# Attention and ternary FFN on one core: PSUM's banks get fixed roles, and exp scores are taken two heads at a time

## The chip, the cores and the metric

One NeuronCore of a Trainium2 chip runs the whole program. Its engines work in parallel, each through its own instructions in order: TensorE (PE) multiplies matrices and writes its results to PSUM, a memory of eight banks (a bank holds 512 float32 numbers in each of 128 partitions); VectorE (DVE) and ScalarE (ACT) read PSUM; GpSimd (POOL) works on the on-chip memory SBUF; SyncE (SP) issues the DMAs. The metric is the device time of one execution in microseconds; the smaller, the better. Runs are given with their median.

## The reference

The input x has 8 sequences of 1024 tokens with 256 features. Cut to what matters here:

```python
x = x + layernorm(attn(layernorm(x), Wq, Wk, Wv, Wo))
x = x + layernorm(ffn(layernorm(x), weight, alpha, bias))

def attn(x, Wq, Wk, Wv, Wo):            # 16 heads of 16, 4 heads of keys and values
    q, k, v = x @ Wq, x @ Wk, x @ Wv    # q and k are then rotated (rope)
    scores = einsum('bhqd,bhkd->bhqk', q, k) / sqrt(256)
    p = softmax(scores, axis=-1)
    return einsum('bhqk,bhkd->bhqd', p, v) @ Wo

def ffn(y, weight, alpha, bias):        # weight is made ternary: -1, 0 or 1
    return einsum('bsd,od->bso', y, ternary(weight) * alpha) + bias
```

The attention is the large part: 8 sequences, 16 heads and 1024 x 1024 scores for each. The softmax subtracts each row's maximum, so the scores are computed twice here: once to find the maxima, and once, with the maxima subtracted inside the matmul, to take the exponentials.

## The kernel before

**Tiling.** The work is cut into `NU` = 16 units of 512 queries (half a sequence). A unit has `G` = 4 blocks, and a block has the four query heads (one of each key-value head) that share a stacked query tile. A block has `NK` = 8 steps, one for each 128 keys, and a step has four score tiles of 128 keys x 512 queries, one for each head. There are 512 steps and 2048 score tiles. Beside them, the maxima pass has 2048 tiles of 128 queries x 512 keys.

The contraction of a score matmul needs only 64 rows of PE: two heads lie in rows 0 to 63 and 64 to 127 (the letter `a` in the code, the row half), and the other two are chosen with `r2`. Two matmuls on different row halves can run at the same time. Queries and keys are split into a high and a low part that are stacked in these 64 rows, and the rows from 48 on hold the maxima with a factor of -1, so that a score comes out shifted.

**The four kinds of work in the loop.**

- `max_scores` (L565): a maxima matmul (L582, `sm`) into a tile of two banks of the pool `ps_mx`, which has two such tiles. DVE reduces both banks together, or each by itself where a window ends between them (`reduce_halves`, L607; `reduce_early`, L612).
- `shift_join` (L620, DVE), `shift_rows` (L626, a transpose on PE and a copy on ACT) and `shift_low` (L635, DVE and two DMAs) bring the maxima of a finished block into the query rows (`q_st<-ml`).
- `exp_one` (L663): an exp matmul (L655, `se`) into one bank of the pool `ps_e`, which has three, and an `Exp` of 128x512 on ACT (L671). In the last 13 steps `exp_two` (L673) uses the two-bank tiles of `ps_mx`.
- `av_piece` (L683): the exponentials times the values (L691, `av`) into the one bank of `ps_av`; `av_out` copies it to SBUF for a DMA to `d_av`.

So PSUM's banks are 2 x 2 for maxima, 3 for exps and 1 for av.

**The other work.** `Project` computes a unit's queries, keys and values three units ahead; `Tail` computes the output projection, the layer norms and the FFN one unit behind. Their parts stand in the lists `P_PARTS`, `L_PARTS` and `T_PARTS` with the step at which each becomes ready. Each of their PE results takes a bank from `psum` (L183): in the loop one of the three of `ps_e`, before and after it also one of the tiles of `ps_mx`.

**The order.** The order of PE, DVE and ACT is written out by hand: instructions are issued as the code calls them. `window` (L1114) issues two or three score tiles' exps, each followed by a maxima matmul, then the ready parts of other work, and last the av matmuls of the window that lies two windows back (`av_windows`). `window_size` (L1055) takes three tiles, or two where a part that needs a PSUM bank is ready; `do_parts` then lets `3 - size` such parts in. `maxima_by` (L1039) says how far the maxima run ahead of the exps: 40 tiles at first, 52 later. `due` holds finished blocks whose shift is to be sent; `collect` makes it ready on whole steps. The exps of a window come out so (L1124 to L1133):

```python
for q in range(max(size, end - maxima[0])):
    if q < size:
        exp_one(s + q)
    if maxima[0] < end:
        max_scores(maxima[0])
        maxima[0] += 1
```

The SP queue issues the DMAs in the order of the program; POOL's order is written by hand at the start and the end, and follows the parts between.

Of the kernel before, what the change touches and what calls it, by code (L numbers as in the profile page):

```python
# [8 lines left out]
F32 = mybir.dt.float32  # L9
F32R = mybir.dt.float32r  # L10
# [18 lines left out]
def kernel(  # L29
# [48 lines left out]
    ep = ctx.enter_context(tc.tile_pool(name="ep", bufs=12))  # L78
    avp = ctx.enter_context(tc.tile_pool(name="avp", bufs=5))
    tailp = ctx.enter_context(tc.tile_pool(name="tailp", bufs=1))  # L80
    dram = ctx.enter_context(tc.tile_pool(name="dram", bufs=3, space=DRAM))
    ps_mx = ctx.enter_context(tc.tile_pool(name="ps_mx", bufs=2, space=PSUM))
    ps_e = ctx.enter_context(tc.tile_pool(name="ps_e", bufs=3, space=PSUM))
# [97 lines left out]
    spare = [1]  # L181

    def psum(shape, name, dtype=F32):  # L183
        if spare[0]:
            spare[0] += 1
            if spare[0] % 5 < 2:
                return ps_mx.tile(shape, dtype, tag="sm", name=name)
        return ps_e.tile(shape, dtype, tag="se", name=name)
# [116 lines left out]
    class Project:  # L305
# [3 lines left out]
        def __init__(self, u, eng):  # L309
            self.u, self.eng = u, eng  # L310
            self.b, self.half = divmod(u, UPB)
            self.xt, self.sc, self.hl = {}, {}, {}
            self.q_rot = None
            if u not in (1, 2):
                xn = qkp.tile([P, UT, D], F32, tag="xn", name=f"xn_{u}", bufs=2)
                xs = qkp.tile([P, 2, UT, D], F32R, tag="hl", name=f"xs_{u}")
                self.xn = [xn[:, 2 * p : 2 * p + 2, :] for p in range(2)]
                self.xs = [[xs[:, l, 2 * p : 2 * p + 2, :] for l in range(2)] for p in range(2)]
            else:
                self.xn = [  # L320
                    tailp.tile([P, 2, D], F32, tag=f"xn{p}", name=f"xn_{u}_{p}") for p in range(2)
                ]
                self.xs = [
                    [ep.tile([P, 2, D], F32R, tag="e", name=f"xs_{u}_{p}_{l}") for l in range(2)]
                    for p in range(2)
                ]

# [67 lines left out]
        def k(self):  # L395

            pt = psum([P, UQ], f"ptk_{self.u}", F32R)
            for t in range(UT):
                nc.tensor.transpose(
                    pt[:, t * P : (t + 1) * P],  # L400
                    self.k_parts[:, t].rearrange("p l d -> p (l d)"),
                    ident_r,
                )
            self.hl["k"] = ep.tile([P, UQ], F32R, tag="e", name=f"hlk_{self.u}")
            nc.scalar.copy(self.hl["k"], pt.bitcast(F32))
# [156 lines left out]
    def head_and_tile(i, r2, t):  # L562
        return r2 * UT + t if i // G < NU - 1 else 2 * t + r2

    def max_scores(v):  # L565


        i, k = divmod(v // 2, 2 * NK)
        u, part = i // G, v % 2
        if i == 0:  # L570
            a, ch, t, r2 = 1 - part, k // NK, k // 2 % UT, k % 2
        else:
            a, ch, t, r2 = 1 - k % 2, part, k // 4, k // 2 % 2
        queries = block_queries(i, r2)
        queries = queries[:, t * P : (t + 1) * P] if u < NU - 1 else queries[:, t]
        if part == 0:
            sm[0] = ps_mx.tile([P, 2, 512], F32, tag="sm", name=f"sm_{i}_{k}")
            if k == 0:
                mx[i] = small.tile([P, 2, 2 * UT, 2], F32, tag="mx", name=f"mx_{i}")
            reduced.clear()  # L580
        rows = slice(64 * a, 64 * a + 64)
        scores = nc.tensor.matmul(  # L582
            sm[0][:, part, :],
            queries[rows],
            k_st[(u // UPB) % 3][rows, r2, ch * 512 : (ch + 1) * 512],
            start=True,
            stop=True,
        )
        if part == 0:
            return  # L590
        if reduced:
            tc.declare_no_dep(scores.ins, early[0], reason="another bank")
        if i == 0:
            nc.vector.tensor_reduce(
                mx[i][:, ::-1, head_and_tile(i, r2, t), ch], sm[0], AX.X, ALU.max
            )
        else:
            reduce_halves(i, k, 2)
        if k == 2 * NK - 1:
            shift_join(i)  # L600
            due.append((v // 4 + (1 if i < 3 else 2), i))

    def reduce_halves(i, k, n):

        lo = len(reduced)
        a, t, r2 = 1 - k % 2, k // 4, k // 2 % 2
        early[0] = nc.vector.tensor_reduce(  # L607
            mx[i][:, a, head_and_tile(i, r2, t), lo:n], sm[0][:, lo:n, :], AX.X, ALU.max
        ).ins
        reduced.extend(range(lo, n))  # L610

    def reduce_early(v):  # L612

        i, k = divmod(v // 2, 2 * NK)
        if i > 0 and v % 2:
            reduce_halves(i, k, 1)

    sm, mhl, shifts, reduced, early = {}, {}, {}, [], [None]
# [44 lines left out]
    def exp_one(s):  # L663

        n, (a, r2) = s // 4, divmod(s % 4, 2)
        assert n // NK in shifts
        i, kt = divmod(n, NK)
        e = es[n, r2, a] = ep.tile([P, UQ], F32, tag="e", name=f"e_{i}_{kt}_{r2}_{a}")
        sc = ps_e.tile([P, 512], F32, tag="se", name=f"se_{i}_{kt}_{r2}_{a}")
        exp_scores(n, r2, a, sc)  # L670
        nc.scalar.activation(e, sc, AF.Exp, scale=1.0 / D**0.5)  # L671

    def exp_two(n, r2):  # L673

        i, kt = divmod(n, NK)
        sc = ps_mx.tile([P, 2, 512], F32, tag="sm", name=f"se_{i}_{kt}_{r2}")
        for a in range(2):
            exp_scores(n, r2, a, sc[:, a, :])
        for a in range(2):
            e = es[n, r2, a] = ep.tile([P, UQ], F32, tag="e", name=f"e_{i}_{kt}_{r2}_{a}")  # L680
            nc.scalar.activation(e, sc[:, a, :], AF.Exp, scale=1.0 / D**0.5)
# [255 lines left out]
    def load(u):  # L937
# [5 lines left out]
        (26, "begin", 0), (33, "x", 0, 0), (34, "x", 0, 1), (37, "begin", 1), (43, "x", 1, 0),  # L943
        (45, "x", 1, 1), (49, "kv_and_dram"), (51, "q", 0), (52, "kt"), (53, "v"), (55, "q", 1),
        (57, "q_to_dram"),
# [8 lines left out]
        (1, "fetch"), (7, "invert"), (8, "scale", 0), (9, "scale", 1), (12, "attn", 0),  # L954
# [4 lines left out]

    P_FIRST = (47, 51, 52, 54, 57, 58, 59, 60, 62, 61, 63, 64)  # L960
# [24 lines left out]
    for k, fs in enumerate((  # L985
# [26 lines left out]
        for f in fs:  # L1012
            at(k - START, *(f if isinstance(f, tuple) else (f,)))
    for u in range(3, NU):
        start = SPU * (u - 4)
        steps = P_FIRST if u == 3 else [k for k, *_ in P_PARTS]
        at(start + steps[0] - 6, load, u)
        if u == 3:
            for k, stage in (
                (7, measure), (9, prepare_wo), (11, add_up), (13, threshold), (15, ternarize),  # L1020
                (22, transpose_ternary),
            ):
                at(k, stage)
        at(start + steps[0] - 1, begin_project, u)
        for k, (_, *p) in zip(steps, P_PARTS):
            at(start + k, part, projects, u, *p)
# [27 lines left out]

    def window_size(s):  # L1055


        left = 4 * NK - s % (4 * NK)
        if s >= ends:
            return 4  # L1060
        if s == 6:
            return 2
        size = min(2 if s >= REGULAR and any(banked(*p) for p in ready) else 3, left, ends - s)
        if left - size == 1:
            size += 1 if size == 2 else -1
        return size

    maxima = [0]

    def collect(n):  # L1070

        if due and due[0][0] <= maxima_by(4 * n + 4) // 4 - 1:
            i = due.pop(0)[1]
            ready.insert(0, (shift_rows, (i,)))
        ready.extend(todo.pop(n, ()))

    def do_parts(banks):

        while ready:
# [14 lines left out]
    def start_step(n):  # L1094
        for q in range(4):
            max_scores(maxima[0])
            maxima[0] += 1
            if q == 1:
                take_low()
        collect(n)  # L1100
        do_parts(99)
# [12 lines left out]
    def window(s):  # L1114
# [5 lines left out]
        if late:  # L1120
            for r2 in range(2):
                exp_two(s // 4, r2)
        else:
            end = min(maxima_by(s + size), 4 * NSTEP)  # L1124
            for q in range(max(size, end - maxima[0])):
                if q < size:
                    exp_one(s + q)
                if maxima[0] < end:
                    max_scores(maxima[0])
                    maxima[0] += 1  # L1130
                if q == 0:
                    take_low()
            reduce_early(maxima[0])  # L1133
# [10 lines left out]
    with tc.manual_schedule(engines={E.PE, E.DVE, E.Activation, E.Pool}):  # L1144
# [40 lines left out]
        spare[0] = 0  # L1185
# [11 lines left out]
        s = 0  # L1197
        while s < 8:
            s = window(s)
# [6 lines left out]
    spare[0] = 1  # L1206
# [69 lines left out]
```

## Time and profile before

| what | value |
|---|---|
| median of 3 runs | 1646.88 us (1641.69 to 1648.25) |
| profiled execution | 1642.63 us |
| its span | 1640.8 us |
| granted PE clock, mean | 0.989 |
| score matmuls: exps (L655), maxima (L582) | 2048, 2048 |
| first and last exp matmul start | 62.7 and 1618.7 us |

The page gives each engine's busy time as a share of the span, then the chain of work that ended last, then groups of equal instructions with the mean time of one. In a line of a group, the part behind the bar has the busy time in us and the mean duration in ns, then the engine's idle time ahead of these instructions and what ended it. A line of waits says: waiting instruction, the one it waited for, total us, times, the longest. A line of the timeline has the start in us, the time in us, the engine, the line in the code and the operation. PEld is PE's weight load, which can overlap a matmul. Some rows merge equal neighbours (x3, x5). A matmul's end is modelled.

From 100 to 1536 us the loop is regular: in each stretch of 100 us PE is busy for 95 to 99 us, DVE for 82 to 91, ACT for 75 to 81, and the granted clock is 1.00.

### The profile page before, as it was taken

What the parts mean: (1) busy time and instruction counts of PE and PEld (TensorE: products, weight loads), DVE (VectorE), ACT (ScalarE), POOL (GpSimd) and SP (SyncE); (2) the same over time, 40 slices, a digit from 0 to 9 for tenths busy, and PEclk for the clock granted to TensorE, in tenths of its full rate; (3) what the DMA queues carried; (4) which work ended last, traced back from release to release, by engine and by line L of the source; (5) the groups of instructions that cost most, each with busy time, mean ns of one, the idle gap of its engine ahead of it and who ended that gap; (6) DMA issues with size and microseconds to landing.
All of it is one profiled execution on the core that took longest, in us unless ns stands there. A gap on an engine that the chain in (4) does not pass through costs nothing.

```text
span 1640.8 us, 37250 instructions
## 1 busy us (share of the span) xinstructions
PE 1579.7 (96%) x14712; PEld 818.5 (50%) x14712; DVE 1399.3 (85%) x2049; ACT 1274.8 (78%) x2479; POOL 835.4 (51%) x1239
## 2 busy tenths in 40 slices
PE   7999999999999999999999999999999999999997
PEld 5544455454545545454544545455454544444544
DVE  7778788889898888989889898988989888898964
ACT  4657778878787887878788787887878787877884
POOL 5532457374653737455373835547374552323363
PEclk8989999999999999999999999999999999999999
DMA  4151425125151422515133251513325151231100
GB/s 139 53 101 34 91 77 101 59 76 101 56 106 49 91 67 82 101 46 105 60 83 75 77 106 44 104 49 89 71 67 104 40 97 42 46 70 34 42 15 27
DMA packets 86079, 117.99 MB, mean 72 GB/s; under 512 B 12088, under 2 KB 50808, under 8 KB 85752
## 3 DMA queue, kind: packets, MB, share of 16 engines
q1 hardware_dynamic: 85904, 115.60, 29.9%
q8 instruction: 116, 1.90, 0.5%
q14 instruction: 59, 0.48, 0.1%
HBM read 68.65 MB, written 45.88 MB: 70 GB/s over the span
## 4 chain that ended last, share of the span: by engine, by line
PE 80%; DVE 10%; DMA 3%; ACT 2%; POOL 2%; issue 2%; SPq 1%; POOLq 0%; DVEq 0%; ACTq 0%
PE av L691 28%; PE se L655 28%; PE sm L582 9%; DVE mx L607 7%; PE pa L283 3%; PE pq L283 2%; PE pf L283 2%; PE pt_ot L267 2%; ACT e L671 2%; PE pt_xt L267 2%; PE pkv L283 2%; DMA q_st<-ml 1%; DMA k_rot<-d_k 1%; PE pm L630 1%; DMA dk<-ks 1%
## 5 line engine op out<-in xcount | busy, mean ns | idle before, releaser
L607 DVE TENSOR_REDUCE mx<-sm 128x2 f32<-128x1024 f32 (+1 forms) x1304 | 1205.3, 973 | 191.9 <-PE sm L582 174.1
L671 ACT ACTIVATE e<-se 128x512 f32<-128x512 f32 x1996 | 1058.2, 602 | 223.0 <-PE sm L582 172.4
L582 PE MATMUL sm<-k_st,q_st 64*128 64x512 f32 x2048 | 748.4, 450 | 6.9 <-DVE mx L607 3.9
L655 PE MATMUL se<-q_st,k_st 64*128 64x512 f32 x2048 | 705.5, 441 | 26.7 <-ACT e L671 14.4
L691 PE MATMUL av<-e,v_aug 128*32 128x256 f32 (+3 forms) x8608 | 607.2, 378 | 0.0
L655 PEld LDWEIGHTS se<-q_st,k_st 64*128 64x128 f32 x2048 | 324.9, 185 | 405.7 <-ACT e L671 302.1
L582 PEld LDWEIGHTS sm<-k_st,q_st 64*128 64x128 f32 x2048 | 326.1, 185 | 65.1 <-DVE mx L607 41.9
L691 PEld LDWEIGHTS av<-e,v_aug 128*32 128x32 f32 x8608 | 194.4, 108 | 211.0 <-issue 148.3
L241 POOL TENSOR_SCALAR lnsc<-mv 128x2 f32<-128x2 f32 (+1 forms) x134 | 25.8, 193 | 400.1 <-DVE mv L239 395.1
L765 POOL TENSOR_TENSOR xn<-xn,a 128x512 f32<-128x512 f32 x30 | 38.4, 1282 | 131.8 <-DMA a<-d_rec 101.2
L826 POOL TENSOR_TENSOR a<-a,bias_bc 128x512 f32<-128x512 f32 x30 | 38.6, 1287 | 108.3 <-ACT a L825 108.3
L242 POOL TENSOR_TENSOR lnsc<-lnsc,mhalf 128x2 f32<-128x2 f32 (+1 forms) x134 | 92.5, 691 | 0.9
L162 POOL TENSOR_TENSOR hl<-xn,hl 128x512 fp32r<-128x512 f32 x60 | 76.5, 1287 | 0.4
L253 POOL TENSOR_SCALAR xn<-x,lnsc 128x256 f32<-128x256 f32 x116 | 65.1, 570 | 2.2
L237 DVE BATCH_NORM_STATS2 bnst<-a 128x6 f32<-128x256 f32 x120 | 44.5, 413 | 4.6 <-POOL a L826 4.6
L297 POOL TENSOR_TENSOR t<-q_rot,sin_q_sb 128x512 f32<-128x512 f32 x31 | 39.9, 1288 | 15.5 <-ACT q_rot L439 15.4
L283 PE MATMUL pa<-woh,hl 128*128 128x256 f32 x240 | 46.2, 294 | 1.1 <-ACT e L671 1.1
L283 PE MATMUL pq<-xt,wqkvh 128*128 128x256 f32 x256 | 45.8, 303 | 0.5 <-ACT e L671 0.5
L237 DVE BATCH_NORM_STATS2 bnst<-x 128x6 f32<-128x256 f32 x124 | 45.9, 412 | 0.4 <-DMA x<-in_L_attn_x 0.4
L271 ACT CAST ot<-pt_ot 128x512 fp32r<-128x512 f32 x66 | 39.6, 601 | 4.7 <-PE pt_ot L267 4.7
L439 ACT COPY q_rot<-pq 128x512 f32<-128x512 f32 x32 | 18.8, 586 | 30.9 <-PE pq L283 30.9
L162 POOL TENSOR_TENSOR hlq<-q_rot,hlq 128x512 fp32r<-128x512 f32 x31 | 39.8, 1285 | 4.8 <-ACT hlq L159 4.5
(157 smaller groups left out, 1303.1 us busy)
## 6 DMA issues: line engine op xcount, KB each, us to landing
q_st<-dq SPq DMA_DIRECT2D x90, 256.0 KB
dq<-hlq SPq DMA_DIRECT2D x60, 256.0 KB
d_av<-avsb SPq DMA_DIRECT2D x60, 256.0 KB
x<-in_L_attn_x SPq DMA_DIRECT2D x15, 512.0 KB
xn<-d_av SPq DMA_DIRECT2D x30, 256.0 KB
a<-d_rec SPq DMA_DIRECT2D x30, 256.0 KB
xr<-in_L_attn_x SPq DMA_DIRECT2D x15, 512.0 KB
out_x<-a SPq DMA_DIRECT2D x30, 256.0 KB
```

The source lines that it names most:

```text
L162: eng.tensor_tensor(lo, src, hi.bitcast(F32), ALU.subtract)
L237: nc.vector.bn_stats(st[:, t, :], src[:, t, :])
L242: nc.gpsimd.tensor_tensor(sc[:, 1, :], sc[:, 1, :], mhalf[:, :n], ALU.pow)
L253: eng.tensor_scalar(dst[:, t, :], src[:, t, :], sc[:, 0, t : t + 1] if eng is nc.gpsimd else mv[:, t, 0:1], sc[:, 1, t : t + 1], ALU.add i ...
L267: nc.tensor.transpose(pt[:, c, t * P : (t + 1) * P], src[:, t, c * P : (c + 1) * P], ident_r)
L283: nc.tensor.matmul(out, chunk(left[i], c), chunk(right[j], c), start=(k == 0), stop=(k == len(steps) - 1),)
L297: eng.tensor_tensor(dst, x, table.unsqueeze(1).to_broadcast(list(x.shape)), ALU.mult)
L582: scores = nc.tensor.matmul(sm[0][:, part, :], queries[rows], k_st[(u // UPB) % 3][rows, r2, ch * 512 : (ch + 1) * 512], start=True, stop= ...
L607: early[0] = nc.vector.tensor_reduce(mx[i][:, a, head_and_tile(i, r2, t), lo:n], sm[0][:, lo:n, :], AX.X, ALU.max).ins
L655: nc.tensor.matmul(sc if len(queries.shape) == 2 else sc.rearrange("p (j t) -> p j t", j=G), k_st[(i // G // UPB) % 3][rows, r2, kt * P : ...
L671: nc.scalar.activation(e, sc, AF.Exp, scale=1.0 / D**0.5)
L691: nc.tensor.matmul(av_ps[0][32 * r : 32 * r + 32, lo:hi], va[:, kt, r, :], es[i * NK + kt, r // 2, r % 2][:, lo:hi], start=(kt == 0 and lo ...
```

## The change

PSUM's eight banks get fixed roles. `ps_mx` is one tile of two banks for maxima (`s2`), `ps_s` is two single banks for maxima (`s1`), `ps_e` has one tile of two banks for exps (`e2`) and one single bank (`se`), and `ps_av` stays. The single bank takes the third exp of a window of three, and in the loop also the PE results of the other work, which run in windows of two.

A window issues, in this order: the exps of two heads into `e2` (two matmuls on alternate row halves, then one `Exp` of 128x1024), two maxima of the two heads into `s2` (then one reduction of both), and in a window of three the third exp into `se` with a single maximum, on the other row half, into `s1`. The queues `pairs` and `singles` hand out the maxima tiles so that each pair and each single gets the row half that it needs. In the last steps `e2` and `s2` both serve exps.

The exponentials lie in two pools: six tiles of two heads (`ep2`) and four of one (`ep`) for twelve of one; `avsb` has two buffers for five. A shift becomes due a number of maxima tiles after its block, not at whole steps, and is looked for in each window. Some parts of `Project` come some steps later, and two of them are placed behind the newest shift's DMA (`behind_latest`).

```diff
-    ep = ctx.enter_context(tc.tile_pool(name="ep", bufs=12))
-    avp = ctx.enter_context(tc.tile_pool(name="avp", bufs=5))
+    ep = ctx.enter_context(tc.tile_pool(name="ep", bufs=4))
+    ep2 = ctx.enter_context(tc.tile_pool(name="ep2", bufs=6))
+    avp = ctx.enter_context(tc.tile_pool(name="avp", bufs=2))
...
-    ps_mx = ctx.enter_context(tc.tile_pool(name="ps_mx", bufs=2, space=PSUM))
-    ps_e = ctx.enter_context(tc.tile_pool(name="ps_e", bufs=3, space=PSUM))
+    ps_mx = ctx.enter_context(tc.tile_pool(name="ps_mx", bufs=1, space=PSUM))
+    ps_s = ctx.enter_context(tc.tile_pool(name="ps_s", bufs=2, space=PSUM))
+    ps_e = ctx.enter_context(tc.tile_pool(name="ps_e", bufs=1, space=PSUM))
...
-    spare = [1]
+    ALONE, ONE = (ps_e, "se"), (ps_s, "s1")
+    PAIR_E, PAIR_M = (ps_e, "e2"), (ps_mx, "s2")
+    spare = [[ALONE, ONE, PAIR_E, ONE, PAIR_M], 0]
...
+    def max_one(a, sm=None):
+        open_block()
+        if not singles[a]:
+            if pairs:
+                for queue in singles:
+                    queue.append(pairs[0])
+                del pairs[0]
+            else:
+                a = 1 - a
+        i, t, r2, ch = item = singles[a].pop(0)
+        if sm is None:
+            sm = ps_s.tile([P, 512], F32, tag="s1", name=f"s1_{a}_{i}_{t}_{r2}_{ch}")
+        max_scores(item, a, sm)
+        x = head_and_tile(i, r2, t)
+        nc.vector.tensor_reduce(mx[i][:, a, x, ch : ch + 1], sm, AX.X, ALU.max)
+        block_ends(i)
+        return a
+
+    def max_two(a, place=None):
+        open_block()
+        pool, tag = place or PAIR_M
+        sm = pool.tile([P, 2, 512], F32, tag=tag, name=f"s2_{taken[0]}")
...
+        i, t, r2, ch = item = pairs.pop(0)
+        for k in range(2):
+            max_scores(item, (a + k) % 2, sm[:, k])
+        x = head_and_tile(i, r2, t)
+        nc.vector.tensor_reduce(mx[i][:, :: -1 if a else 1, x, ch], sm, AX.X, ALU.max)
+        block_ends(i)
...
-    def exp_one(s):
...
-        sc = ps_e.tile([P, 512], F32, tag="se", name=f"se_{i}_{kt}_{r2}_{a}")
-        exp_scores(n, r2, a, sc)
+    def exps_of(s, n, place=None):
+        pool, tag = place or (ALONE if n == 1 else PAIR_E)
+        shape = [P, 2, 512] if n == 2 else [P, 512]
+        sc = pool.tile(shape, F32, tag=tag, name=f"se_{s}")
+        e = (ep2 if n == 2 else ep).tile(shape, F32, tag=f"e{n}", name=f"e_{s}")
+        for k in range(n):
+            step, (r2, a) = (s + k) // 4, divmod((s + k) % 4, 2)
...
+            exp_scores(step, r2, a, sc[:, k] if n == 2 else sc)
         nc.scalar.activation(e, sc, AF.Exp, scale=1.0 / D**0.5)
...
-            due.append((v // 4 + (1 if i < 3 else 2), i))
+            due.append((taken[0] + (3 if i < 3 else 6), i))
...
     P_PARTS = (
-        (26, "begin", 0), (33, "x", 0, 0), (34, "x", 0, 1), (37, "begin", 1), (43, "x", 1, 0),
-        (45, "x", 1, 1), (49, "kv_and_dram"), (51, "q", 0), (52, "kt"), (53, "v"), (55, "q", 1),
-        (57, "q_to_dram"),
+        (30, "begin", 0), (35, "x", 0, 0), (36, "x", 0, 1), (37, "begin", 1), (43, "x", 1, 0),
+        (45, "x", 1, 1), (49, "kv_and_dram"), (51, "q", 0), (54, "kt"), (53, "v"), (55, "q", 1),
+        (62, "q_to_dram"),
...
+            behind = [behind_latest] if u > 4 and p[0] in ("kt", "q_to_dram") else []
...
-            end = min(maxima_by(s + size), 4 * NSTEP)
-            for q in range(max(size, end - maxima[0])):
-                if q < size:
-                    exp_one(s + q)
-                if maxima[0] < end:
-                    max_scores(maxima[0])
-                    maxima[0] += 1
...
+            n = max(0, min(maxima_by(s + size), 4 * NSTEP) - taken[0])
+            exps_of(s, 2)
+            take_low()
+            half = s % 2
+            if n >= 2:
+                max_two(half)
+                n -= 2
+            if size == 3:
+                exps_of(s + 2, 1)
+            else:
+                half = 1 - half
+            while n:
+                if n == 2:
+                    max_two(1 - half)
+                    break
+                half = max_one(1 - half)
+                n -= 1
...
+    spare[0] = [ALONE]
```

## The prediction

> **What bounds the kernel now.** I read the page's shares first, then the groups of instructions with shapes kept apart, the waits, and a stretch of the timeline.
>
> ```profile
> PE 1579.7 (96%) x14712; PEld 818.5 (50%) x14712; DVE 1399.3 (85%) x2049; ACT 1274.8 (78%) x2479; POOL 835.4 (51%) x1239
> PE 80%; DVE 10%; DMA 3%; ACT 2%; POOL 2%; issue 2%; SPq 1%; POOLq 0%; DVEq 0%; ACTq 0%
> ```
>
> PE holds 80% of the chain that ended last, but its 96% busy is modelled from pipelined matmuls, so it doesn't say that PE never waits. DVE is the next engine.
>
> ```profile
> L671 ACT ACTIVATE e<-se 128x512 f32<-128x512 f32 x1996 | 1058.2, 602 | 223.0 <-PE sm L582 172.4 <-PE se L655 31.8
> L607 DVE TENSOR_REDUCE mx<-sm 128x2 f32<-128x1024 f32 x712 | 855.3, 1216 | 167.5 <-PE sm L582 153.2 <-PE se L655 11.0
> L607 DVE TENSOR_REDUCE mx<-sm 128x1 f32<-128x512 f32 x592 | 381.9, 680 | 24.5 <-PE sm L582 20.9
> ```
>
> Of DVE's 1399 us, 1237 are maxima. A reduction of two banks lasts 1216 ns, one of one bank 680; started back to back in the trace they follow each other after 1.132 and 0.598 us (medians). The exps last 602 ns and follow each other after 0.491.
>
> ```profile
> PE se L655 <- ACT e L671: 14.4, 32, 0.5
> PE se L655 <- DMA q_st<-ml: 9.9, 8, 3.1
> PE pt_ot L267 <- ACT e L671: 6.9, 14, 0.5
> PEld sm L582 <- DVE mx L607: 41.9, 127, 1.4
> ```
>
> PE loses little to ACT by the first and third lines, and 9.9 us to the DMA of the shifts by the second; the fourth shows where it meets DVE.
>
> ```profile
> 801.33 0.49 PE L582 MATMUL sm<-k_st,q_st 64*128 64x512 f32 x1
> 801.94 0.18 PEld L582 LDWEIGHTS sm<-k_st,q_st 64*128 64x128 f32 x1 [0.23 <-DVE mx L607]
> 801.94 0.49 PE L582 MATMUL sm<-k_st,q_st 64*128 64x512 f32 x1
> 802.27 0.39 PE L582 MATMUL sm<-k_st,q_st 64*128 64x512 f32 x1
> 806.24 0.50 PE L655 MATMUL se<-q_st,k_st 64*128 64x512 f32 x1
> 806.78 1.58 ACT L671 ACTIVATE e<-se 128x512 f32<-128x512 f32 x3 [0.58 <-PE sm L582]
> 807.04 4.68 DVE L607 TENSOR_REDUCE mx<-sm 128x2 f32<-128x1024 f32 x5 [0.82 <-PE sm L582]
> ```
>
> At 801.94 a maxima matmul waits for a bank that DVE still reads. It starts with its weights unloaded and lasts 0.49 us, where the next one, at 802.27, lasts 0.39. DVE starts about 0.07 after the end of the last matmul it needs (the median of such starts), and PE goes on about 0.05 after DVE's end. From 806.24 (exp matmul) to 806.78 (ACT) it is 0.53.
>
> The loop runs in windows: 441 of three score tiles and 313 of two between the start-up and the last 13 steps. From the start of each window's first exp matmul in the trace, a window of three takes 1.806 us on average (half of them under 1.7) and one of two 2.164; together 796 + 677 us. DVE's maxima in a window of three need 0.598 + 1.132 = 1.73 us. So windows of 1.5 to 1.7 us run ahead of DVE: four banks in two tiles hold the lead, and longer windows, such as those of 2.3, pay it back. **DVE sets the mean pace of the windows of three, PE that of the single window.**
>
> **The change, part by part.**
>
> *Maxima.* The code gives each window of three one reduction of two banks and one of one; of two, one of two banks. Over the program that is 790 of two banks and 468 of one (counted in the built program), where before there were 728 and 592. By the intervals: before 728 x 1.132 + 592 x 0.598 = 1178 us, after 790 x 1.132 + 468 x 0.598 = 1174. DVE's work stays.
>
> What goes is its lead. The two-bank tile for maxima is now single. Its loop: the waiting pair of matmuls 0.49, to DVE's start 0.07, reduction 1.216, to PE 0.05: 1.83 us, once per window, whether of three or two (every window begins with the exp pair and then this pair). The single bank's reduction, issued behind it, covers most of that for DVE, not all: 1.83 - 1.73 = 0.10 us of DVE idle per window of three, 441 x 0.10 = **+44 us**. This is not hidden: queued behind the waiting pair on PE are the third exp's matmul, the single maximum's and all of the window's av matmuls, and ACT waits for the third exp. The bounds: if only the mean counted, a floor of 1.83 over 1.806 costs 441 x 0.024 = 11 us. If each window of three that was shorter than 1.83 is stretched to it and nothing is paid back, the 300 such windows lose 61 us. I take 44, since a window's lead over DVE's 1.73 was borrowed anyway.
>
> Windows of two: DVE needs only 1.132 there, but 123 of them were shorter than 1.83, by 31 us in sum. Bounds 0 and 31; I take half, **+16**, since some of the short ones are followed by a long one of the same DVE queue.
>
> A rule that speaks against the change stands in the Trainium skill (Perfetto Trace Analysis, Optimizing Tensor Performance): independent matmul groups should rotate through different PSUM banks, so that the evacuation of one overlaps the matmuls of the next. Taken strictly, nothing here overlaps any longer and the sum would be the full 61 + 31 us; the trace's row, a 0.598 reduction behind the 1.132 one, says that most of the gap is covered.
>
> *Exps.* 1996 exps of one bank become 770 of two and 456 of one, and the 52 last ones become 26 pairs. A 128x1024 exp is not in the trace. ACT's copies out of PSUM last 373 ns at 256 wide and 587 at 512, so 512 more cost 428: 602 + 428 = 1.03 us, and the next starts 0.491 + 0.428 = 0.919 after it. Bounds: 0.86 (the slope alone) and 1.204 (two of today's). ACT's own work falls by 796 x (0.982 - 0.919) = 50 us. That is not on the path: ACT is 78% busy. What it can bring is PE's waits for ACT, 14.4 + 6.9 us and some tenths in smaller lines; I take **-20** of the 0 to -24. The loop of the single two-head exp tile is 0.53 + 1.03 + 0.05 = 1.61 us, below the 1.83 of the maxima; with the far bound of 1.204 it is 1.79, still below. If the maxima's loop were gone, the exps' loop would be next: at 1.62, 148 windows of the trace were shorter, by 20 us in all.
>
> The skill's page ScalarE: Activation LUTs (What ACT_TABLE_LOAD costs) has 186 ns + 0.833 ns per element and an overlap of 93 ns, so 1.04 and 0.95 us as an estimate; that leaves the loop below the maxima's and changes the sum by nothing.
>
> *The bank shared with other work.* Projections, transposes and the shifts' transpose now take the one bank of the third exp. They run in windows of two, which have no third exp, as before. Two in a row: the second's matmuls stand behind av (0.57 us for two tiles in the trace), an exp pair and a maxima pair (0.34 + 0.23, start to start), 1.14 us; the first's evacuation needs 0.07 + 0.59 + 0.05 = 0.71. Covered, at nothing. Without the cover, 102 pairs of such windows x 0.71 = 72 us.
>
> *At nothing:* the row halves alternate within each pair, where before an exp and a maximum made a pair; matmuls and av stay the same in number (2048, 2048). Sixteen e tiles of 512 where 12 were. Two avsb buffers for five: a block writes one, and a block lasts eight steps, some 24 us, against a DMA of a few. Projection parts a few steps later: 3 to 5 steps are 9 to 15 us, and what they feed (stacked queries, keys) is used over 30 steps later; their POOL operations, the keys' and queries' DMAs on SP's queue come behind the shift's two DMAs instead of ahead, which frees those. The exps wait for the shift's DMA today for 9.9 us in 8 waits; the shift now goes out 6 tiles behind its block instead of 8, -2 us at best; I count 0.
>
> **Sum:** 44 + 16 - 20 = +40 on the profiled execution's 1642.6 (span 1640.8 and 1.8 around it): 1682.6. That execution is 4.3 under the median of the runs shown, 1646.9; on the median: **1687 us**.
>
> **Rivals.**
>
> *ACT's relief decides (faster).* If windows are released by ACT, a window of three needs 0.919 + 0.491 = 1.41 instead of 1.473, one of two 0.919 instead of 0.982: 754 x 0.063 = -48 us, 1599. For it: 302.1 us in which the weight loads of exps wait for ACT. Against: most of that overlaps av still running on PE, PE's own line is 14.4, and DVE's total doesn't fall. It decides if the maxima's loop stays under some 1.65, which needs DVE to free banks before the end of its record. Chance 0.13.
>
> *All is paid back (no change).* The mean of 1.806 is already the DVE's pace; the floor costs 11 and ACT's relief gives 20: -9, 1638. With windows of two losing half of theirs it is +7, 1654. Chance 0.10.
>
> *Nothing is paid back (slower by far).* 61 + 31 = +92 without relief: 1739. For it: long windows hold their own work, such as projections' matmuls on PE, and can't be shortened. Against: in the windows of 2.3 us DVE is busy throughout, which is its queue being emptied. Chance 0.15.
>
> The forecast, a single tile that costs DVE 0.1 us per window, has 0.62, its own range 1665 to 1710. That the change doesn't do what it says is excluded by the built program's counts. The range of 1650 to 1728 leaves out the faster case and the far half of the last. A measurement can tell about 0.5%, 8 us, from no change. Slower 0.62 + 0.15 = 0.77, same 0.10, faster 0.13.
>
> **What would show it.** Right: maxima matmuls of the two-bank tile waiting for DVE in most windows; two-bank reductions starting 1.8 us apart in runs of windows of three; PE's waits for exps nearly gone; exps of 1024 near 1.03 us; ACT less busy by some 50 us, DVE's busy time within 1%. Wrong: windows of three under 1.75 in the median (the release is earlier than I take it), exps of 1.2 us (then they bind too), or other work's matmuls waiting for the shared bank.

## The result, and the profile after

The changed kernel takes 1694.67 us (median of 4 runs, 1691.89 to 1698.02) against 1646.95 (4 runs, 1641.69 to 1648.25): 1.0297 times as long, with a 95% interval of 1.0267 to 1.0327. The forecast was 1687, slower, with a range of 1650 to 1728.

The page's shares and the chain of the changed kernel (its line numbers are some 10 to 30 higher: exps L695, maxima of two banks L638 and of one L621, maxima matmuls L598):

```profile
span 1691.6 us, 36139 instructions
PE 1609.5 (95%) x14456; PEld 777.6 (46%) x14456; DVE 1419.0 (84%) x1987; ACT 1231.1 (73%) x1683; POOL 834.7 (49%) x1239
PE 59%; DVE 30%; ACT 6%; issue 2%; POOL 2%; DMA 2%; SPq 0%; ACTq 0%; POOLq 0%; DVEq 0%
```

The chain shows it first: DVE's share went from 10% to 30%, PE's from 80% to 59%. DVE's busy time hardly moved (1399 to 1419 us), so more work alone did not put it there. The groups, shapes apart:

```profile
L638 DVE TENSOR_REDUCE mx<-s 128x2 f32<-128x1024 f32 x790 | 964.8, 1222 | 226.5 <-PE s L598 220.6 <-PE se L676 3.0
L695 ACT ACTIVATE e<-se 128x1024 f32<-128x1024 f32 x796 | 816.4, 1028 | 307.2 <-PE se L676 300.7 <-PE s L598 0.9
L621 DVE TENSOR_REDUCE mx<-s 128x1 f32<-128x512 f32 x468 | 317.9, 680 | 5.5 <-PE s L598 3.6 <-PE se L676 1.9
```

A reduction takes what it took (1222 and 680 ns), but DVE now sits idle for 226.5 us ahead of those of two banks (167.5 before) and for almost nothing ahead of those of one. An exp of two heads lasts 1028 ns. The waits:

```profile
ACT e L695 <- PE se L676: 304.2, 670, 3.4
DVE mx L638 <- PE s L598: 220.6, 307, 4.7
PEld s L598 <- DVE mx L638: 170.3, 562, 1.8
PE s L598 <- DVE mx L638: 24.9, 55, 1.3
```

The weight loads of maxima matmuls wait for DVE 562 times (127 before), and DVE then waits for the matmuls: each for the other, around one tile. One turn of it in the timeline:

```profile
804.90 0.50 PE L598 MATMUL s<-k_st,q_st 64*128 64x512 f32 x2 [0.16 <-DVE mx L638]
805.24 0.39 PE L676 MATMUL se<-q_st,k_st 64*128 64x512 f32 x1
805.45 1.23 DVE L638 TENSOR_REDUCE mx<-s 128x2 f32<-128x1024 f32 x1
805.57 0.64 PE L705 MATMUL av<-e,v_aug 128*32 128x256 f32 x8
806.59 0.68 DVE L621 TENSOR_REDUCE mx<-s 128x1 f32<-128x512 f32 x1
806.73 0.19 PEld L598 LDWEIGHTS s<-k_st,q_st 64*128 64x128 f32 x2 [0.41 <-DVE mx L638]
806.73 0.50 PE L598 MATMUL s<-k_st,q_st 64*128 64x512 f32 x2
807.27 1.23 DVE L638 TENSOR_REDUCE mx<-s 128x2 f32<-128x1024 f32 x1
```

From 804.90 to 806.73 is the forecast loop of 1.83 us: matmuls 0.50, the two-bank reduction from 805.45 to 806.67, and PE goes on 0.05 later. The reduction of one bank, begun at 806.59, ends at 807.27, as the next pair is ready; in this turn DVE has no gap, and the two-bank reductions are still 1.82 us apart. The turn is typical: from 400 to 1500 us there are 548 intervals between the starts of two-bank reductions, 294 of them from 1.81 to 1.83 us and only one under 1.78.

The starts of the exp matmuls in the trace give the time of each unit (128 score tiles; units are numbered from 0), and this is the finest measure of all that follows, since start-up and last steps stay out of it. It is taken from one profiled execution of each kernel. The ten middle units (3 to 12) are alike to within 1.1 us before and 0.3 us after; units 13 and 14 have no projections any more.

| us per unit | before | after |
|---|---|---|
| units 3 to 12, mean | 96.69 | 100.57 |
| of it in 28 windows of three, 22 of two | 49.4 + 47.2 | 51.4 + 49.2 |
| DVE busy, idle (units 4 to 11) | 85.1, 11.5 | 86.4, 14.2 |
| ACT busy, idle (units 4 to 11) | 78.3, 18.3 | 75.5, 25.1 |
| DVE idle in windows of three, of two (units 3 to 12) | 6.5, 5.1 | 6.8, 7.4 |
| units 13 and 14 | 92.93 | 93.61 |

Over the regular windows, 3-tile windows went from 796 to 827 us and 2-tile ones from 677 to 698: +52, all of the span's +51. An engine's busy and idle time together are the time, so the row on DVE only divides the 4.0 us by which units 4 to 11 got longer: 2.7 are idle time of DVE, and 1.3 are busy time, which is overlap between its instructions that was lost.

### The profile page after: what moved, and what is told of

Its sections match the earlier page's. It is cut to its first block, busy times and chain, and to the rows that moved or that the text cites. A ratio compares the mean times of both kernels' runs of the same rounds, so it can differ in the third digit from the quotient of the medians.

```text
span 1691.6 us, 36139 instructions
## 1 busy us (share of the span) xinstructions
PE 1609.5 (95%) x14456; PEld 777.6 (46%) x14456; DVE 1419.0 (84%) x1987; ACT 1231.1 (73%) x1683; POOL 834.7 (49%) x1239
## 4 chain that ended last, share of the span: by engine, by line
PE 59%; DVE 30%; ACT 6%; issue 2%; POOL 2%; DMA 2%; SPq 0%; ACTq 0%; POOLq 0%; DVEq 0%
DVE mx L638 19%; PE av L705 19%; PE se L676 15%; PE s L598 12%; DVE mx L621 6%; ACT e L695 5%; PE pa L296 3%; PE pq L296 3%; DVE bnst L250 2%; PE pt_ot L280 2%; PE pkv L296 1%; PE pf L296 1%; PE pt_xt L280 1%; DVE mv L252 1%; DMA xr<-in_L_attn_x 1%
## 5 line engine op out<-in xcount | busy, mean ns | idle before, releaser
L695 ACT ACTIVATE e<-se 128x1024 f32<-128x1024 f32 (+1 forms) x1252 | 1042.1, 870 | 318.0 <-PE se L676 304.2
L638 DVE TENSOR_REDUCE mx<-s 128x2 f32<-128x1024 f32 x790 | 964.8, 1222 | 226.5 <-PE s L598 220.6
L705 PE MATMUL av<-e,v_aug 128*32 128x256 f32 (+3 forms) x8352 | 615.0, 385 | 0.0
L676 PE MATMUL se<-q_st,k_st 64*128 64x512 f32 x2048 | 578.2, 474 | 20.6 <-ACT e L695 6.5
L598 PE MATMUL s<-k_st,q_st 64*128 64x512 f32 x2048 | 488.8, 453 | 38.8 <-DVE mx L638 24.9
L676 PEld LDWEIGHTS se<-q_st,k_st 64*128 64x128 f32 x2048 | 233.5, 184 | 386.1 <-ACT e L695 284.6
L621 DVE TENSOR_REDUCE mx<-s 128x1 f32<-128x512 f32 x468 | 317.9, 680 | 5.5 <-PE s L598 3.6
L598 PEld LDWEIGHTS s<-k_st,q_st 64*128 64x128 f32 x2048 | 211.6, 185 | 182.6 <-DVE mx L638 170.3
L705 PEld LDWEIGHTS av<-e,v_aug 128*32 128x32 f32 x8352 | 188.6, 108 | 228.2 <-issue 156.6
```

What stands on the lines that cost most here:

```text
L598: nc.tensor.matmul(sm, queries[rows], keys, start=True, stop=True)
L621: nc.vector.tensor_reduce(mx[i][:, a, x, ch : ch + 1], sm, AX.X, ALU.max)
L638: nc.vector.tensor_reduce(mx[i][:, :: -1 if a else 1, x, ch], sm, AX.X, ALU.max)
L676: nc.tensor.matmul(sc if len(queries.shape) == 2 else sc.rearrange("p (j t) -> p j t", j=G), k_st[(i // G // UPB) % 3][rows, r2, kt * P : ...
L705: nc.tensor.matmul(av_ps[0][32 * r : 32 * r + 32, lo:hi], va[:, kt, r, :], es[i * NK + kt, r // 2, r % 2][:, lo:hi], start=(kt == 0 and lo ...
```

## The experiments

**The two halves of the change, each alone.** PSUM's eight banks allow both mixes. The first keeps the change's exps and takes back before's maxima:

```diff
-    ps_mx = ctx.enter_context(tc.tile_pool(name="ps_mx", bufs=1, space=PSUM))
-    ps_s = ctx.enter_context(tc.tile_pool(name="ps_s", bufs=2, space=PSUM))
+    ps_mx = ctx.enter_context(tc.tile_pool(name="ps_mx", bufs=2, space=PSUM))
...
+            for _ in range(min(2, n)):
+                max_next()
+                n -= 1
+            if size == 3:
+                exps_of(s + 2, 1)
+            for _ in range(n):
+                max_next()
+            reduce_early()
```

> The exp part of the change alone: exps in one tile of two heads and one single bank, maxima back in two rotating tiles of two banks, each bank reduced by itself where a window ends between them. Theory (the single maxima tile's loop of 1.83 us costs the time): the loss goes, ACT's relief stays, 1630 to 1652 us. Rival (the single two-head exp tile is what binds, loop 1.61 us and no lead for ACT): stays at 1680 to 1700 us.

Measured: 1657.45 us (1.0083 times before, 1.0068 to 1.0098), 97.8 us per unit. Some three quarters of the loss are gone. The wait between PE and DVE is back to its old size:

```profile
PEld s L597 <- DVE mx L616: 55.3, 117, 1.5
```

But the time is 5 us over the range of the theory: ACT's relief did not come, and this mix is still slower than the kernel before.

The second mix keeps the change's maxima and takes back the three single banks for exps:

```diff
-    ps_e = ctx.enter_context(tc.tile_pool(name="ps_e", bufs=1, space=PSUM))
+    ps_e = ctx.enter_context(tc.tile_pool(name="ps_e", bufs=3, space=PSUM))
...
+            sc = pair[:, k] if place else ps_e.tile([P, 512], F32, tag="se", name=f"se_{s + k}")
+            exp_scores(step, r2, a, sc)
...
+            nc.scalar.activation(e, sc, AF.Exp, scale=1.0 / D**0.5)
```

> The maxima part of the change alone: one tile of two banks and two single banks for maxima, exps of one bank each in three rotating banks, other work in these three. Theory (maxima tile): as slow as the whole change or slower by ACT's relief, 1690 to 1720 us. Rival (exp tile): back near 1647, at most 1660 us.

Measured: 1748.16 us, above both expectations. The unit times tell why: this mix starts its first exp at 83.9 us (61.9 in the change) and needs 131.5 us for the last unit (93.2), with one two-bank tile where the change has two for its start and its last 13 steps. PE waits for ACT there, and the granted clock is lower (0.79 from 1595 to 1726 us, against 1.00 in the change's last unit). In the middle it takes 100.57 us per unit, to the hundredth the changed kernel's time. So in the loop the maxima part, with the change's order and dates, costs what the whole change costs.

**Order alone.** The third mix has neither tile role (its maxima are issued as in the first mix, its exps as in the second): three single exp banks and two rotating maxima tiles, but the change's order in a window, its dates of shifts and its steps of projections.

```diff
-    ps_e = ctx.enter_context(tc.tile_pool(name="ps_e", bufs=1, space=PSUM))
+    ps_e = ctx.enter_context(tc.tile_pool(name="ps_e", bufs=3, space=PSUM))
...
-    ps_mx = ctx.enter_context(tc.tile_pool(name="ps_mx", bufs=1, space=PSUM))
-    ps_s = ctx.enter_context(tc.tile_pool(name="ps_s", bufs=2, space=PSUM))
+    ps_mx = ctx.enter_context(tc.tile_pool(name="ps_mx", bufs=2, space=PSUM))
```

> PSUM as before (three single banks for exps, two rotating maxima tiles), but with the change's order within a window (two exps, two maxima, the third exp, the third maximum, heads alternating), its dates of the shifts and its steps of the projections. Revised theory (the two single tiles cost the time, the order nothing): 96.2 to 97.2 us per unit in the middle, as before (96.7). Rival (the order of exps and maxima costs): 97.5 or more, as with the exp part alone (97.7).

Measured: 97.34 us per unit, between the two expectations (1692.23 us in all, since its last unit takes 141.7 us: in the last 13 steps its matmuls and exps alternate within a two-bank tile, PE waits 23.9 us for ACT there, and the granted clock is 0.81). With it the table of the loop is complete:

| us per unit, units 3 to 12 | two maxima tiles | one maxima tile and two single banks |
|---|---|---|
| three single exp banks | 97.34 | 100.57 |
| one exp tile of two heads and a bank | 97.79 | 100.57 |

The kernel before, with its own order, has 96.69. So of +3.88, the order, the dates and the moved steps together have 0.65, the maxima's tile 2.8 to 3.2, and the exps' tile 0.0 to 0.45. (The moved steps alone, put into the kernel before, make +0.51, as shown below, so the order of exps and maxima may have little of the 0.65.)

**Maxima in four single banks.** The same four banks, but rotating one by one, each reduced by itself:

```diff
-    ps_mx = ctx.enter_context(tc.tile_pool(name="ps_mx", bufs=1, space=PSUM))
-    ps_s = ctx.enter_context(tc.tile_pool(name="ps_s", bufs=2, space=PSUM))
+    ps_s = ctx.enter_context(tc.tile_pool(name="ps_s", bufs=4, space=PSUM))
...
+    def max_two(a):
+        for half in (a, 1 - a):
+            max_one(half)
```

> The change, but with the maxima in four rotating single banks and a reduction of one bank each (2048 of them). DVE gets more work: 790 x (2 x 0.598 - 1.132) = 51 us, 1.79 us per window of three. Theory (maxima tile's loop): banks come free one by one, the wait goes, most of the 51 us shows, 1660 to 1685 us. Rival (DVE's total work sets the time): 1694 + 51, about 1745 us. Rival (exp tile): no gain, 1695 or more.

Measured: 1679.93 us (1.0215, 1.02 to 1.023), 98.25 us per unit. DVE is busy for 1433.0 us, more than the change's 1419.0, and the loop is faster by 2.3 us per unit; here too the last unit is longer (108.6 us). This is against DVE's total work as the cause, and for the way its banks come free.

**The moved steps.** The change with the projection steps of before (none placed behind the newest shift, and the tail's fetch one step earlier, as before):

```diff
-        (30, "begin", 0), (35, "x", 0, 0), (36, "x", 0, 1), (37, "begin", 1), (43, "x", 1, 0),
-        (45, "x", 1, 1), (49, "kv_and_dram"), (51, "q", 0), (54, "kt"), (53, "v"), (55, "q", 1),
-        (62, "q_to_dram"),
+        (26, "begin", 0), (33, "x", 0, 0), (34, "x", 0, 1), (37, "begin", 1), (43, "x", 1, 0),
+        (45, "x", 1, 1), (49, "kv_and_dram"), (51, "q", 0), (52, "kt"), (53, "v"), (55, "q", 1),
+        (57, "q_to_dram"),
...
-            behind = [behind_latest] if u > 4 and p[0] in ("kt", "q_to_dram") else []
-            at(start + k, *behind, part, projects, u, *p)
+            at(start + k, part, projects, u, *p)
```

> The change with the projection parts back at the steps of before and not placed behind the newest shift. Theory (PSUM roles cost the time, moved steps nothing): 1688 to 1701 us. Rival (the moved parts collide with other work): 1680 us or less.

Measured: 1705.48 us (1.0371, 1.0355 to 1.0386). It fits neither expectation: the moved steps are not at nothing, they save the change some 11 us. That raised the question whether they would help the kernel before, which would have beaten both, with the same steps put into it:

```diff
...
-        (57, "q_to_dram"),
+        (62, "q_to_dram"),
...
+            behind = [behind_latest] if u > 4 and p[0] in ("kt", "q_to_dram") else []
+            at(start + k, *behind, part, projects, u, *p)
```

> The kernel before with the moved projection steps alone (and their placing behind the newest shift). In the change these steps are worth about 11 us (1705 with the old ones, 1694 with the new). If they help whatever the PSUM roles are: 1632 to 1640 us, faster than both kernels. If they only fit the changed windows: 1642 to 1655 us.

Measured: 1650.72 us (1.0032, 1.0017 to 1.0046), 97.20 us per unit against 96.69. They cost some 4 to 5 us there, so of the two kernels they help the changed one alone.

**The shared bank.** Other work in the single maxima's two banks instead of the third exp's:

```diff
-        spare[0] = [ALONE]
+        spare[0] = [ONE]
```

> The change, but in the loop the other work takes the two single banks of the maxima instead of the third exp's bank. Theory (the single two-bank maxima tile costs the time; the shared bank costs nothing): 1688 to 1700 us. Rival (sharing the third exp's bank costs): 1685 us or less.

Measured: 1690.21 us, within the theory's range; 100.58 us per unit in the middle, as the change (100.57). The 4 us lie in the first unit, 115.0 against 119.1. In the loop the shared bank costs nothing.

**DVE out of the way.** In both kernels every maxima reduction reads half of its scores, so half of the keys are left out of the maxima. For the kernel before:

```diff
-                mx[i][:, ::-1, head_and_tile(i, r2, t), ch], sm[0], AX.X, ALU.max
+                mx[i][:, ::-1, head_and_tile(i, r2, t), ch], sm[0][:, :, :256], AX.X, ALU.max
...
-            mx[i][:, a, head_and_tile(i, r2, t), lo:n], sm[0][:, lo:n, :], AX.X, ALU.max
+            mx[i][:, a, head_and_tile(i, r2, t), lo:n], sm[0][:, lo:n, :256], AX.X, ALU.max
```

> The kernel before, with every maxima reduction reading only the first 256 of a bank's 512 scores (half of the keys are left out of the maxima). DVE's need in a window of three falls from 1.73 to about 0.93 us, so it should be PE's own work that sets the pace: about 1.65 us for a window of three, 1560 to 1620 us in all.

And for the changed one:

```diff
-        nc.vector.tensor_reduce(mx[i][:, a, x, ch : ch + 1], sm, AX.X, ALU.max)
+        nc.vector.tensor_reduce(mx[i][:, a, x, ch : ch + 1], sm[:, :256], AX.X, ALU.max)
...
-        nc.vector.tensor_reduce(mx[i][:, :: -1 if a else 1, x, ch], sm, AX.X, ALU.max)
+        nc.vector.tensor_reduce(mx[i][:, :: -1 if a else 1, x, ch], sm[:, :, :256], AX.X, ALU.max)
```

> The changed kernel with the same half reductions (half of the keys left out of the maxima). The maxima tile's loop falls from 1.83 to about 1.29 us, below the 1.62 of the exp tile. Theory (maxima tile's loop): the 48 us between the kernels shrink to between -10 and +20 us against e8a. Rival (the two-head exp tile, the window's order or the shared bank): 40 us or more remain.

Measured: 1587.24 and 1619.75 us. The difference shrinks from 48 to 32.5, not below 20. The theory as I had it, with one loop, falls. DVE binds no more (55% busy in the changed kernel with half reductions); that kernel's waits:

```profile
DVE mx L638 <- PE s L598: 635.6, 729, 4.2
PEld se L676 <- ACT e L695: 380.4, 824, 1.7
ACT e L695 <- PE se L676: 252.0, 587, 4.4
```

DVE waits ahead of nearly each two-bank reduction (729 of 790); PE and ACT wait for each other. Three single exp banks show much the same wait (342.8 us, 820 times, in the second mix with half reductions, below), so that row alone does not name the exps' tile; the shortest windows do. In units 3 to 14, no window of the changed kernel is shorter than 1.61 us here (the forecast loop of the exps' tile), while of before's 594 windows with half reductions 156 are under 1.5. Its timeline has such a turn:

```profile
800.32 0.50 PE L676 MATMUL se<-q_st,k_st 64*128 64x512 f32 x2
800.64 0.59 ACT L718 COPY avsb<-av 128x512 f32<-128x512 f32 x1
801.11 1.54 ACT L695 ACTIVATE e<-se 128x1024 f32<-128x1024 f32 x2
802.21 0.19 PEld L676 LDWEIGHTS se<-q_st,k_st 64*128 64x128 f32 x2 [0.77 <-ACT e L695]
802.82 1.03 ACT L695 ACTIVATE e<-se 128x1024 f32<-128x1024 f32 x1 [0.17 <-PE se L676]
```

The pair written at 800.32 waits in PSUM until ACT has copied an av result, the two-head exp (the first of the two merged ones) runs from 801.11 for 1.06, and only then PE may write the tile again, at 802.21: 1.89 us for this window. So the theory became: two single tiles, two loops, and the longer one shows. The two mixes from above, each with half reductions, tested it. Exps of the change with two maxima tiles:

```diff
-            out, src = mx[i][:, ::-1, x, ch], half_done[1]
+            out, src = mx[i][:, ::-1, x, ch], half_done[1][:, :, :256]
...
-            out, src = mx[i][:, 1 - lo, x, ch : ch + 1], half_done[1][:, lo]
+            out, src = mx[i][:, 1 - lo, x, ch : ch + 1], half_done[1][:, lo, :256]
```

> Exps of the change, the two rotating maxima tiles of before, and half reductions (half of the keys left out of the maxima), so that DVE binds nowhere. Revised theory (a second loop, that of the single two-head exp tile with its floor of 1.62 us, is what is left of the difference): 1605 to 1625 us, as the changed kernel with half reductions (1620). Rival (the maxima tile still binds at half reductions): back to the 1587 us of the kernel before with half reductions.

Three single exp banks with the maxima of the change, whose reductions are edited as in the changed kernel:

> Exps of one bank each in three banks, maxima of the change, half reductions (half of the keys left out of the maxima). Its whole time also holds the longer start and last 13 steps that this mix showed with full reductions, so it is read by units of 128 score tiles. Revised theory (exp tile): 93 to 95 us per unit in the middle, as the kernel before with half reductions (93.7). Rival (maxima tile): 96 to 97.5, as the changed kernel with half reductions (96.8).

Measured: the first takes 1618.28 us, as expected by the revised theory, and 96.62 us per unit against 96.78 with both tiles single and 93.72 for the kernel before. The second takes 1643.82 us in all, with a longer start and last unit as in the full version, and 95.26 per unit, just over its range of 93 to 95: below the rival's, but not as low as the kernel before, from which it differs in the order too. The shortest windows agree: of the 594, none is under 1.61 us in the first, and 125 are under 1.5 in the second. So with DVE relieved, the exps' tile costs 1.5 us per unit (95.26 to 96.78), and the maxima's tile 0.2 beside it (96.62 to 96.78). The other 1.5 (93.72 to 95.26) is the order and the maxima's tile together, and was not split.

**One maxima tile in the kernel before.**

```diff
-    ps_mx = ctx.enter_context(tc.tile_pool(name="ps_mx", bufs=2, space=PSUM))
+    ps_mx = ctx.enter_context(tc.tile_pool(name="ps_mx", bufs=1, space=PSUM))
```

> The kernel before with one two-bank maxima tile instead of two, and nothing else changed. Theory (a tile's loop of 1.83 us: 0.49 matmuls, 0.07 to DVE, 1.216 reduction, 0.05 back): 64 tiles per unit, so 64 x 1.83 = 117 us per unit in the middle where it was 96.7, about 1950 us in all. If PE gets its bank back before the reduction has ended, or other work hides the loop: 105 us per unit or less, under 1800.

Measured, in a single execution: 2894.25 us, some 168 per unit, far beyond the theory's figure. One stretch of its busy times (length, then PE, PEld, DVE, ACT and POOL, the granted clock, DMA share, GB/s), its granted clock in 40 slices (tenths), and two turns of its timeline:

```profile
1500.00:1700.00 200.00, 169.98 (x1063) 76.50 (x1063) 104.39 (x142) 94.97 (x176) 59.66 (x89) 0.73 0.22 48
PEclk6555686576777868787786858777596866656668
```

```profile
1499.89 0.50 PE L582 MATMUL sm<-k_st,q_st 64*128 64x512 f32 x1 [1.12 <-DVE mx L607]
1500.32 0.86 PE L691 MATMUL av<-e,v_aug 128*32 128x128 f32 x16
1500.43 0.69 DVE L607 TENSOR_REDUCE mx<-sm 128x1 f32<-128x512 f32 x1 [0.59 <-PE sm L582]
1501.11 0.50 PE L582 MATMUL sm<-k_st,q_st 64*128 64x512 f32 x1
1501.68 0.69 DVE L607 TENSOR_REDUCE mx<-sm 128x1 f32<-128x512 f32 x1 [0.56 <-PE sm L582]
1502.43 0.49 PE L582 MATMUL sm<-k_st,q_st 64*128 64x512 f32 x1 [0.59 <-DVE mx L607]
1506.52 0.79 PE L582 MATMUL sm<-k_st,q_st 64*128 64x512 f32 x1 [1.08 <-DVE mx L607]
```

A tile that is split by the end of a window takes from 1499.89 (its first matmul) to 1502.43, 2.54 us: two reductions in turn, and between them the second matmul stands behind the av matmuls. And PE, now idle so often, is granted 0.73 of its clock in this stretch; at 1506.52 a maxima matmul lasts 0.79 where it lasted 0.49. The loop of 1.83 was reckoned for a tile that is filled and reduced whole, at the full clock; I had left out both of these.

No version that takes all keys into the maxima beats the kernel before.

## Why the prediction was right, and where it wasn't

*The loop of the maxima tile.* Right, to the hundredth: 1.83 us, 804.90 to 806.73, and the signs that were named came: waits of maxima matmuls for DVE in most windows (562 waits, 754 regular windows), two-bank reductions 1.8 us apart, windows of three at 1.82 us in the median. It is the cause of most of the loss: the mixes give it 2.8 to 3.2 of the 3.9 us per unit.

*+44 in windows of three, +16 in windows of two.* The sum of 60 stands against +31 and +21, 52 measured, which already has the exps' part in it. In place it was wrong. I had put 0.10 us of DVE idle into each window of three, as if they ran in steady rows, 2.8 us for the 28 of a unit. In units 3 to 12 DVE's idle time in them rose by 0.2 us per unit, and in the windows of two by 2.3. Units 13 and 14, with 34 windows of three and 13 of two each, should have lost 3.4 us by that; they lost 0.7. There the windows of three were at DVE's pace before too: 1.90 us in the mean (1.92 after), with DVE busy for 91% of them, and half reductions take 7.1 us off such a unit of the kernel before, against 3.0 off a middle one. In units 3 to 12, where other work comes between, they were at 1.77 and went to 1.84. What the second tile gave was a lead that DVE could work off during the windows of two, while PE does projections; with one tile, the lead ends with the window, and DVE stands idle in the windows of two. Runs with a steady row alone were not made; this reading rests on the two kinds of units and on where DVE's idle time lies.

*-20 from ACT's relief.* This is the term that failed. Its means were right: exps of 1028 ns (1.03 forecast), following each other after 0.921 us (0.919), ACT 44 us less busy (50 forecast), and PE's plain waits for exps 6.5 us instead of 14.4. But nothing of it reached the end: with the maxima's tile in place, pairing the exps changes the unit by 0.00, and without it by +0.45. With DVE relieved the two-head tile costs 1.5 us per unit, so its own loop takes away at least what it saves in ACT's time; how much each is by itself, no run shows. With -20 set to 0, the sum would have been 1707; the loss of windows, put at 60 where 52 were measured with everything in, made up for it in part. That 1687 came within 8 us of 1695 is in so far luck.

*"The exps' loop would be next, 20 us".* Right in order, and in price as far as the runs tell: with DVE relieved, 32.5 us remain between the kernels. Units 3 to 14 differ by 37 us, and of these the exps' tile has 21 (1.5 in each of the first ten, 2.9 in each of the last two, against the second mix). The other 16 lie with the order, the steps and the maxima's tile, for which I had no price there.

*The moved steps at nothing.* Wrong: -11 us in the change, +4 in the kernel before. I had looked for a wait of the exps for their results. What they shift is where windows of two fall: in unit 7 of the change, windows of three come six in a row at the start, and with the old steps three. That I did not cost; why it helps one kernel and not the other stays open.

*The shared bank at nothing; its cover.* Right in the loop (100.58 against 100.57), 4 us in the first unit.

*The alternating row halves at nothing.* The order, dates and steps together cost 0.65 us per unit; how much of it is the row halves was not split.

*DVE's busy time within 1%.* 1.4%: reductions less often overlap their neighbour. Before, 494 of 592 one-bank reductions had not ended when DVE's next instruction began; after, 187 of 468.

*The rivals.* ACT's relief as the faster case fell with the first mix, which is freed of the maxima's loop and still slower than before. "All is paid back" (1638 to 1654) fell with the result. "Nothing is paid back" (1739) asked for 92 us; 52 were lost.

## What to carry to other kernels

A PSUM tile's worth is the loop fill, hand over, read, hand back; with one tile this loop was a floor under the time from reduction to reduction here (1.83 us; windows, counted from their first exp, can be shorter, 251 of the 594 in units 3 to 14 are under 1.82), and with two it was a lead that an engine at 85% could use in stretches where PE does something else. Before merging two banks into one larger tile, compute that loop from the rows, compare it with the shortest windows and not with the mean, and do so for each tile that becomes single: here the next longest loop took over when the first one was relieved. ACT's 44 us of saved busy time were worth nothing to the whole, since its tile was not the one being waited for.

## What the runs showed of the hardware

With one maxima tile in the kernel before, PE waited often and its clock fell with it. PE was idle for 15% of the time between 150 and 2750 us (3% in the middle of the changed kernel), in gaps of 0.65 us in the mean and never over 1.4. The mean granted clock was 0.72, where the kernel before and the changed one had 0.99, and a maxima matmul went from 0.49 to 0.79 us. That is a part of the 1250 us lost, where the loop alone had been reckoned at 300; how large a part was not split.

The trace ties the two together. Its clock is granted in steps of 3.4 us, each at full speed or at half. The 107 falls from full to half came after a step in which PE had been idle for 35% in the mean, the 106 returns after a step with almost no idle time (0.1% in the mean), and full speed was kept after steps with 18% in the mean. So no long gap was needed, and the clock came back after steps without waits. It is one execution of one kernel; the lower clocks in the last units of the second and third mixes (0.79 and 0.81) come with waits of PE too.

The other part was the order: in the turn at 1499.89, av matmuls stand ahead of a tile's second maxima matmul, which starts at 1501.11, 0.68 us after the reduction of the first began, and so hold up the second reduction until 1501.68.
